# Four 64x64 tiles for the score columns of a graph-attention kernel, from a copy with exchanged partition halves, at the end of the step

## The chip, the cores and the metric

The kernel runs on one core of one Trainium2 chip. The metric is the device time of one launch in microseconds (us), the median of several runs. A profile is one further execution; its span goes from the first to the last instruction and leaves out what lies around them.

## The reference, cut to what matters

Eight batches of 2048 nodes with 64 channels go through two graph-attention layers under one mask (a random adjacency plus the diagonal), then a leaky ReLU, a layer norm with gamma and beta, the residual and a second layer norm.

```python
def _gat_layer(h, mask, b):
    scores = jnp.einsum('...nd,...md->...nm', h, h)
    scores = jnp.where(mask, scores, NEG)
    attn = jax.nn.softmax(scores, axis=-1)
    return jnp.einsum('...nm,...md->...nd', attn, h) + b
h = jnp.einsum('bnc,hdc->bhnd', x, Wh)              # 4 heads of 64
out_h = _gat_layer(h, mask[None, None], bh[None, :, None, :])
z = jax.nn.leaky_relu(cat, negative_slope=0.2)      # cat: the heads side by side
h2 = jnp.einsum('bnk,dk->bnd', z, Wo)
out2 = _gat_layer(h2, mask[None], bo)
z2 = jax.nn.leaky_relu(out2, negative_slope=0.2)
out = layernorm(z2) * gamma + beta
x = layernorm(x + out)
```

## The kernel before

The adjacency is sparse apart from the first 59 nodes ("hubs"). The other 1989 nodes are split into 153 sets of 13. For each set the kernel finds the up to 128 neighbours of its members, gathers their rows from a table in DRAM with an indirect DMA, and does the attention of the set on that block. The 8 batches stand as 4 pairs (Q), the two batches of a pair in the two halves of the 128 partitions (channels 0 to 63 of the one, 64 to 127 of the other).

A score of layer 1 is x_n' (Wh' Wh) x_m for each head. So the kernel first multiplies the own rows of a set by the 64x64 matrix Wh'Wh of each head. These products are the **score columns**. `gram` holds the four matrices as 128x128 blocks with the same 64x64 matrix in both diagonal quarters and zeros elsewhere, so that one 128x128 matmul serves both batches of a pair.

Layer 1 runs as one loop of steps i, each for a group of two sets (77 groups). All order is written by hand; the engines execute their own instructions in that order and wait for each other by semaphores. A step does, for several groups at different stages:

- `scores(i + 1)` (L901): 32 matmuls of 64x64 tiles, gathered rows against the columns y; `weigh` (L906, VectorE) subtracts the mask, `lift` (L913, ScalarE) takes exp.
- `project` (L579): the heads' weights on the attention output of group i - 1, 64x64 tiles, into the PSUM tile `cat`; `leaky` (L566, ScalarE) moves it to z, `leak` (L571, VectorE) follows.
- the ScalarE copies of the two transposed banks to xTg (L1235).
- `values(i)` (L927) into `o`; `invert` (L934, L935, VectorE) divides by the sums into `osb`.
- `second_maps` (L961) and `second_rows` (L971), both into other columns of `cat`; VectorE keeps them with `keep_own` (L966) and `keep_rows` (L975), and two DMAs on SP's queue store the rows in the second layer's table (L978).
- `columns(i + 4)` (L886): two matmuls (four records, for fp32 takes two passes) of 128x128 tiles on 208 columns into `cat`; `keep_columns` (L892, ScalarE) copies them to y.
- `turn` of the rows of the group three on, first set (L560, four transposes into bank 0), `turn_values(i)` (L944, four transposes of `osb`), `keep_values` (L951, two ScalarE copies), `turn` of the second set (L560, bank 1).

On every even step GpSimd makes the own rows of four sets (`own_rows`, L880, tile `xo`, two buffers), for the columns of the step two on and of the one after it. `cat` has one buffer: the next step's `project` writes into it only when all readers of the last one are through.

SP's queue issues DMAs in order. From step 30 on every even step adds the twelve or so loads of own rows of x (L1010) and the store of the last ones with beta (L1015) to the two row stores of each step; the loads wait until the store from the same buffer, issued just ahead of the last two row stores, has landed. Before that step it has the row stores, and in the first steps the rest of the adjacency loads.

## Time and profile before

| | |
|---|---|
| median of 3 runs | 963.1 us (962.69 to 968.35) |
| span of the profiled execution | 828.9 us, granted TensorE clock 0.974 |
| difference of median and span, outside the profile | 134.2 us |
| busy share: TensorE matmul, VectorE, ScalarE, GpSimd | 87%, 72%, 64%, 54% |
| chain that ended last: TensorE, VectorE, DMA | 61%, 13%, 12% |
| layer 1 loop | from 138.6 us to about 566 us of the span |
| a regular step of it | 5.13 to 5.14 us |

The page has no time of the profiled execution other than the span; the times of runs are device times of other executions. A row of the timeline reads: start, duration, engine, line, operation, tile written <- tiles read, shape of the tile and of the operands, count, and in brackets the idle time ahead and what ended it. The end of a matmul is modelled, so neighbouring rows overlap by a little; starts are recorded. A row of the chain reads: start, time charged, what. "PEld" is the load of the weights.

### The profile page before, as it was taken

How to read it: one execution, taken by the hardware profiler on the slowest of the kernel's cores; microseconds unless marked ns; L12 is line 12 of the kernel's file. 1: busy time of each engine (PE TensorE's matmuls, PEld its weight loads, DVE VectorE, ACT ScalarE, POOL GpSimd, SP SyncE). 2: the span in 40 equal slices, each digit the busy share in tenths (PEclk: the TensorE clock that was granted, in tenths of full speed). 3: DMA queues.
4: the chain of work that ended last, by engine and by line, in shares of the span. 5: the costliest groups of instructions: out<-in, count | busy, mean ns of one | idle time of the engine just before them, and what ended most of it. 6: DMA issues, size and time to landing. Idle time of an engine off the chain costs nothing.

```text
span 828.9 us, 40381 instructions
## 1 busy us (share of the span) xinstructions
PE 725.0 (87%) x17262; PEld 615.5 (74%) x17262; DVE 600.8 (72%) x1328; ACT 529.3 (64%) x1131; POOL 449.9 (54%) x620
## 2 busy tenths in 40 slices
PE   1998688889999999999999999998999899989820
PEld 1675457678788889898989889887787688877620
DVE  3446984568778877898767777764347999998883
ACT  0354445556666667667667667773667899988852
POOL 5455356456445455555545555512777777777600
PEclk9999999999999999999999999999999999999975
DMA  4988744343323333454545545532986667766621
GB/s 83 231 225 240 219 156 111 98 121 98 86 71 90 96 90 98 119 144 139 143 120 141 142 139 137 142 114 88 300 245 185 192 170 214 224 201 197 172 54 32
DMA packets 80262, 121.55 MB, mean 147 GB/s; under 512 B 34539, under 2 KB 50751, under 8 KB 80075
## 3 DMA queue, kind: packets, MB, share of 16 engines
q0 software_dynamic: 24752, 65.67, 29.4%
q1 hardware_dynamic: 50973, 52.11, 21.6%
q8 instruction: 138, 2.26, 1.1%
q10 hardware_dynamic: 4350, 1.10, 0.7%
q14 instruction: 49, 0.40, 0.2%
HBM read 116.81 MB, written 18.25 MB: 163 GB/s over the span
## 4 chain that ended last, share of the span: by engine, by line
PE 61%; DVE 13%; DMA 12%; ACT 5%; issue 4%; SPq 3%; POOL 1%; POOLq 0%; DVEq 0%; ACTq 0%
PE s L901 10%; PE o L927 10%; PE bank L560 8%; PE cat L886 6%; DMA raw<-in_adj_dram 4%; PE o L944 4%; PE cat L579 4%; PE cat L961 4%; PE t L560 3%; PE bank L1343 2%; SPq L1461 2%; PE cat L971 2%; PE o L1373 2%; DMA rows<-table,index 2%; DMA out_dram<-y_s 2%
## 5 line engine op out<-in xcount | busy, mean ns | idle before, releaser
L872 POOL DMA_INDIRECT g<-table,index x154 | 162.3, 1054 | 172.8 <-PE o L927 145.5
L872 POOL DMA_INDIRECT rows<-table,index x153 | 161.2, 1053 | 51.8 <-issue 18.6
L566 ACT ACTIVATE z<-cat,bhp 128x208 f32<-128x208 f32 x154 | 58.4, 430 | 101.7 <-PE cat L579 101.7
L906 DVE TENSOR_TENSOR e<-s,mask 128x832 f32<-128x832 f32 x77 | 78.6, 1020 | 28.4 <-PE s L901 27.6
L927 PE MATMUL o<-g,e 128*64 128x65 f32 x2464 | 92.3, 226 | 5.6 <-issue 5.5
L560 PE MATMUL t<-ident,rows 128*128 128x128 f32 x612 | 86.1, 278 | 10.0 <-DMA rows<-table,index 4.7
L560 PE MATMUL bank<-ident,g 128*128 128x128 f32 x616 | 92.3, 273 | 1.5 <-DVE e L1106 1.2
L927 PEld LDWEIGHTS o<-g,e 128*64 128x64 f32 x2464 | 80.1, 138 | 17.1 <-issue 6.9
L901 PE MATMUL s<-y,xTg 64*64 64x52 f32 x4928 | 88.7, 220 | 0.0
L901 PEld LDWEIGHTS s<-y,xTg 64*64 64x64 f32 x4928 | 78.9, 134 | 12.9 <-issue 12.9
L1497 ACT COPY xts<-t 128x512 f32<-128x512 f32 x153 | 82.2, 583 | 7.0 <-PE t L560 6.0
L1235 ACT COPY xTg<-bank 128x512 f32<-128x512 f32 x154 | 82.6, 596 | 2.4 <-PE bank L560 2.4
L560 PEld LDWEIGHTS t<-ident,rows 128*128 128x128 f32 x612 | 66.5, 140 | 23.0 <-issue 9.9
L913 ACT ACTIVATE e<-e,shifts 128x832 f32<-128x832 f32 x77 | 78.4, 1019 | 2.0 <-DVE e L906 2.0
L742 POOL TENSOR_SCALAR a<-raw 117x1024 bf16<-117x1024 int32 x34 | 38.7, 1140 | 71.5 <-DMA raw<-in_adj_dram 49.1
L560 PEld LDWEIGHTS bank<-ident,g 128*128 128x128 f32 x616 | 73.5, 140 | 4.9 <-issue 1.3
L657 ACT ACTIVATE e<-e,shifts 128x960 f32<-128x960 f32 x32 | 35.1, 1096 | 54.7 <-DVE e L654 49.0
L886 PE MATMUL cat<-xo,gram 128*128 128x208 f32 (+1 forms) x304 | 66.3, 341 | 0.8 <-issue 0.8
L951 ACT COPY otb<-o 128x208 f32<-128x208 f32 x154 | 43.8, 335 | 22.0 <-ACT y L892 10.9
L654 DVE TENSOR_TENSOR e<-sh,maskh 128x960 f32<-128x960 f32 x32 | 36.9, 1154 | 26.6 <-PE sh L650 17.2
L935 DVE TENSOR_TENSOR osb<-o,rall 128x512 f32<-128x512 f32 x77 | 53.2, 692 | 2.7
L934 DVE RECIPROCAL rall<-o 64x8 f32<-64x8 f32 x154 | 31.5, 204 | 31.7 <-PE o L927 30.2
(198 smaller groups left out, 1488.0 us busy)
## 6 DMA issues: line engine op xcount, KB each, us to landing
raw<-in_adj_dram SPq DMA_DIRECT2D x34, 432.0 KB
xr_s<-table SPq DMA_DIRECT2D x19, 256.0 KB
table<-x SPq DMA_DIRECT2D x16, 260.0 KB
table<-rowt SPq DMA_DIRECT2D x152, 26.4 KB
out_dram<-y_s SPq DMA_DIRECT2D x152, 24.0 KB
x<-in_x_dram SPq DMA_DIRECT2D x24, 128.0 KB
table<-xb SPq DMA_DIRECT2D x11, 256.0 KB
table<-share SPq DMA_DIRECT2D x10, 256.0 KB
```

Of the source, the lines that this page charges most:

```text
L560: nc.tensor.transpose(tp[:, q * P:(q + 1) * P], rows[:, q, 1:1 + P], ident)
L566: nc.scalar.activation(z[:, hp], cat[:, :, hp * n:(hp + 1) * n], AF.Identity, bias=bhp[:, hp:hp + 1], scale=1.0)
L872: nc.gpsimd.indirect_dma_start(out=t.rearrange("n q c -> n (q c)"), out_offset=None, in_=table, in_offset=bass.IndirectOffsetOnAxis(ap=ind ...
L886: nc.tensor.matmul(cat[:, k, :n], gram[:, g % 2 * 2 + k, :], held["x", g // 2][:, :n], start=True, stop=True)
L901: nc.tensor.matmul(sp[half(r), p, (q * 2 + j) * M:(q * 2 + j + 1) * M], xt[half(p), j, q, half(r)], y[half(p), (j * Q + q) * M:(j * Q + q ...
L906: nc.vector.tensor_tensor(e[:, :16 * M].rearrange("p (a q n) -> p a q n", a=2, q=Q), sp[:, :, :8 * M].rearrange("p a (q n) -> p a q n", q= ...
L913: nc.scalar.activation(e[:, :16 * M], e[:, :16 * M], AF.Exp, bias=shifts[:, 0:1], scale=1.0)
L927: nc.tensor.matmul(op[half(p), j, o0:o0 + K1], e[:, c0:c0 + 64], rw[j][:, q, sums(p)], start=True, stop=True)
L935: nc.vector.tensor_tensor(osb, v[:, :, :, 1:K1], r.unsqueeze(3).to_broadcast([P, 4, 2, D]), OP.mult)
L951: nc.scalar.copy(ot.rearrange("c h (p w n) -> c p h w n", p=2, w=4)[:, p], v[:, :, p * 64:p * 64 + M].rearrange("c w (n h) -> c h w n", h=H))
L1235: nc.scalar.copy(t[:, k, :], bank[k])
L1497: nc.scalar.copy(xts[pair(s) % 4][:, s % 2, :], tp)
```

## The change

The columns of a head pair are made by four 64x64 matmuls in place of two 128x128 ones, one for each head and each batch of the pair. Head k of the pair reads row half k of the array and writes PSUM bank k, for both output halves p. Where k and p are the same half, the moving data are the own rows `xo` as they stand; where they differ, they come from `xs`, a copy of `xo` with the two partition halves exchanged. `swap_rows` makes that copy with two DMAs on SP's queue (each 64 partitions of 832 bytes), at the end of every odd step, for the columns of the next step and of the one after it. `xs` has one buffer. The columns and their copy to y move from the middle of the step, behind `second_rows`, to its end, behind the second `turn`. To make room, two tiles of the hub nodes take parts of a shared tile in place of buffers of the work pool.

```diff
+    def swap_rows(m):
+        n = quad(m)[1] * Q * SET
+        t = held["xs", m] = work.tile([P, 2 * GM], F32, tag="xs", name=f"xs{m}", bufs=1)
+        for k in range(2):
+            nc.sync.dma_start(out=t[half(k), :n], in_=held["x", m][half(1 - k), :n])
...
+    def columns_by_halves(g, cat):
+        n = quad(g // 2)[1] * Q * SET
+        for off in range(2):
+            for k in range(2):
+                p = k ^ off
+                nc.tensor.matmul(cat[half(p), k, :n], gram[half(k), g % 2 * 2 + k, half(k)],
+                                 held["xs" if off else "x", g // 2][half(k), :n], start=True, stop=True)
...
+    swap_rows(1)
...
             second_rows(i - 3, pr)
-        if 2 <= i + 4 < NG + NG % 2:
-            columns(i + 4, cat)
-            keep_columns(i + 4, cat)
...
             turn(bank[1], rows[1, 2 * (i + 3) + 1])
+        if 2 <= i + 4 < NG + NG % 2:
+            columns_by_halves(i + 4, cat)
+            keep_columns(i + 4, cat)
+            if i % 2 and i + 5 < NG + NG % 2:
+                swap_rows((i + 5) // 2)
```

TensorE in an even step of the loop before, from the second layer's maps to the next scores (`cat` is the PSUM tile of projection, maps and columns, `o` that of the values, `bank` those of the transposed rows, `g` gathered rows):

```order
L961 MATMUL cat_8030<-z_7930,woT 64x2x4x13 [waits Activation_49]
L961 MATMUL cat_8030<-z_7930,woT 64x2x4x13 x3
L971 MATMUL cat_8030<-ident,own_7975 104x128
L886 MATMUL cat_8030<-xo_7840,gram 128x208 [waits Pool_49]
L886 MATMUL cat_8030<-xo_7840,gram 128x208
L560 MATMUL bank_1919<-ident,g_106_7832 128x128 [waits DMASW7_49,Activation_49]
L560 MATMUL bank_1919<-ident,g_106_7832 128x128 x3
L944 MATMUL o_8046<-ident,osb_8063 128x116 [waits DVE_49]
L944 MATMUL o_8046<-ident,osb_8063 128x116 x3
L560 MATMUL bank_1920<-ident,g_107_7836 128x128 [waits DMASW0_49,Activation_49]
L560 MATMUL bank_1920<-ident,g_107_7836 128x128 x3
L901 MATMUL s_8124<-y_7862,xTg_8042 64x52 [waits PE_49]
```

The same place in the changed kernel (its lines L976, L986, L900, L959 and L916 are the maps, the rows, the columns, the turned values and the scores):

```order
L976 MATMUL cat_8211<-z_8106,woT 64x2x4x13 x3
L986 MATMUL cat_8211<-ident,own_8148 104x128
L560 MATMUL bank_1919<-ident,g_106_8006 128x128 [waits DMASW7_49,Activation_49]
L560 MATMUL bank_1919<-ident,g_106_8006 128x128 x3
L959 MATMUL o_8227<-ident,osb_8244 128x116 [waits DVE_49]
L959 MATMUL o_8227<-ident,osb_8244 128x116 x3
L560 MATMUL bank_1920<-ident,g_107_8010 128x128 [waits DMASW0_49,Activation_49]
L560 MATMUL bank_1920<-ident,g_107_8010 128x128 x3
L900 MATMUL cat_8211<-xo_8014,gram 64x208 [waits DVE_49,Pool_49]
L900 MATMUL cat_8211<-xo_8014,gram 64x208
L900 MATMUL cat_8211<-xs_8174,gram 64x208 [waits DMAHW1_49]
L900 MATMUL cat_8211<-xs_8174,gram 64x208 [waits DMAHW2_49]
```

The columns went from between `second_rows` and the first transposes to behind the second ones; between `second_rows` and the transposes of `osb` only four transposes are left. The second pair of matmuls waits for the two DMAs of the copy; in odd steps it has no wait of its own.

SP's queue in the changed kernel, from step 30 on, from the row stores of an even step to the loads of the next one (`rowt` are rows for the second layer's table, `table_174` takes the own rows with beta, `xb` is one of the two tiles for own rows):

```order
L993 DMA table_99<-rowt_113 4x13x130 [waits DMAHW4_49,DVE_49]
L993 DMA table_99<-rowt_113 4x13x130 [waits DMAHW5_49]
L1030 DMA table_174<-xb 128x512 [waits DMAHW6_49,DVE_49]
L993 DMA table_99<-rowt_114 4x13x130 [waits DMAHW7_49,DVE_49]
L993 DMA table_99<-rowt_114 4x13x130 [waits DMAHW0_49]
L886 DMA xs_8174<-xo_8014 64x208 [waits DMAHW1_49,PE_49,Pool_49]
L886 DMA xs_8174<-xo_8014 64x208 [waits DMAHW2_49]
L1025 DMA xb<-in_x_dram 12x2x256 [waits DMAHW6_49,DMAHW3_49]
```

The two DMAs of `xs` are new, between the odd step's row stores and the next loads; the rest is as before. The first of them waits for TensorE, which must be through with the last `xs`, and the loads behind it still wait for the store into `table_174` to land.

ScalarE, before and then changed, from the exp of a step to the next step's projection:

```order
L913 ACTIVATE e_111<-e_111,shifts 128x832 [waits DVE_49,Activation_49]
L892 COPY y_8572<-cat_8505 128x208x2 [waits PE_49]
L951 COPY otb_8590<-o_8521 128x4x52 [waits DVE_49,PE_49,Activation_49]
L951 COPY otb_8590<-o_8521 128x4x52
L566 ACTIVATE z_8640<-cat_8631,bhp 128x208 [waits PE_49]
```

```order
L928 ACTIVATE e_111<-e_111,shifts 128x832 [waits DVE_49,Activation_49]
L966 COPY otb_8536<-o_8471 128x4x52 [waits DVE_49,PE_49,Activation_49]
L966 COPY otb_8536<-o_8471 128x4x52
L907 COPY y_8547<-cat_8455 128x208x2 [waits DVE_49,PE_49]
L565 ACTIVATE z_8592<-cat_8583,bhp 128x208 [waits PE_49]
```

The copy of the columns to y went from ahead of the two copies of the turned values to behind them, so it is the last thing that ScalarE reads from `cat` before the next projection writes there.

## Prediction

> **What bounds the kernel now.** First the page: the engines' busy shares and the chain that ended last.

> ```profile
> PE 725.0 (87%) x17262; PEld 615.5 (74%) x17262; DVE 600.8 (72%) x1328; ACT 529.3 (64%) x1131; POOL 449.9 (54%) x620
> PE 61%; DVE 13%; DMA 12%; ACT 5%; issue 4%; SPq 3%; POOL 1%; POOLq 0%; DVEq 0%; ACTq 0%
> ```

> TensorE is the busiest engine and most of the chain, but over the whole span. So the chain inside the loop comes next, for one regular step.

> ```profile
> 403.16 1.08 PE s L901 x64
> ...
> 404.24 0.37 PE cat L579 x16
> 404.61 1.08 PE o L927 x32
> ...
> 406.32 0.71 PE cat L886 x4
> 407.02 0.44 PE bank L560 x4
> 407.46 0.40 PE o L944 x4
> ...
> 408.30 1.08 PE s L901 x64
> ```

> The step is TensorE from end to end: 408.30 - 403.16 = 5.14 us, of which the columns (L886) are 0.71. If nothing else moved, every 0.1 us off TensorE's work would be 0.1 us off the step. The timeline of the same step says whether something else stands close behind.

> ```profile
> 404.54 1.15 PE L927 MATMUL o<-g,e 128*64 128x65 f32 x32
> ...
> 405.74 0.42 DVE L934 RECIPROCAL rall<-o 64x8 f32<-64x8 f32 x2 [0.41 <-PE o L927]
> ...
> 406.15 0.87 PE L886 MATMUL cat<-xo,gram 128*128 128x208 f32 x4
> 406.20 0.69 DVE L935 TENSOR_TENSOR osb<-o,rall 128x512 f32<-128x512 f32 x1
> ...
> 407.30 0.56 PE L944 MATMUL o<-ident,osb 116*128 116x116 f32 x4
> ...
> 407.69 0.60 PE L560 MATMUL bank<-ident,g 128*128 128x128 f32 x4
> ...
> 408.23 0.39 PE L901 MATMUL s<-y,xTg 64*64 64x52 f32 x11
> ```

> VectorE waits for the end of the values (L927), takes two reciprocals and the division into osb, and is through at 406.20 + 0.69 = 406.89. TensorE reads osb at 407.30 (L944). So the slack is 0.41 us, and it exists because the columns (L886, 0.71 in the chain) lie between. **The second bound is this path, values, reciprocals, osb, turned values, and it starts and ends on TensorE.**

> The trace shows what happens without that cover. Late in the loop the columns are half as wide, and then there are none.

> ```profile
> 542.21 1.15 PE L927 MATMUL o<-g,e 128*64 128x65 f32 x32
> ...
> 543.82 0.59 PE L886 MATMUL cat<-xo,gram 128*128 128x104 f32 x4
> ...
> 544.68 0.26 PE L944 MATMUL o<-ident,osb 116*128 116x116 f32 x1
> ...
> 551.92 1.15 PE L927 MATMUL o<-g,e 128*64 128x65 f32 x32
> ...
> 554.33 0.61 PE L944 MATMUL o<-ident,osb 116*128 116x116 f32 x4 [0.63 <-DVE osb L935]
> ```

> From the start of the values to the turned values it is 407.30 - 404.54 = 2.76 us in a regular step, 2.47 with half columns and 2.41 with none, where TensorE waits for osb. The last figure doesn't depend on what TensorE has to do meanwhile: **2.41 us is the floor.** (In that case the four transposes of bank 0 are missing too; they are 0.44 in the chain, less than the 0.63 of the wait without them, so with them the floor stands.)

> **The change, part by part.** *Taking the columns out of the middle.* TensorE's work there falls by 0.71, but the leg falls only from 2.76 to 2.41: a gain of 0.35 us a step, and a new wait for osb of about 0.35. That wait replaces the cover.

> *Refilling after the wait.* [...] After the wait the next operation's matmul starts 560.14 - 559.69 = 0.45 behind the first turned value, against 407.69 - 407.30 = 0.39 in the regular step: 0.06 lost.

> ```profile
> 559.69 0.61 PE L944 MATMUL o<-ident,osb 116*128 116x116 f32 x4 [0.63 <-DVE osb L935]
> 560.14 0.27 PE L1174 MATMUL bank<-share,own 128*117 128x120 f32 x1
> ```

> *The columns at the end.* Four matmuls of 64x64 tiles, 208 columns, two records each: 8 records. The projection is 16 records of 104 columns in the same four quarters of the array, as many record columns, and the chain above charges it 0.37. The hub scores are the nearest row in width:

> ```profile
> 127.43 1.04 PE L650 MATMUL sh<-share,xT 64*64 64x240 f32 x16
> L650 PE MATMUL sh<-share,xT x512: 362/363/660, 28.4 to 130.5; 64*64 64x240 f32 x171
> ```

> Sixteen records of 240 columns, the last one 0.36 long: three groups of four in 0.68, 0.23 a group, and 2 groups x 0.23 x 208/240 = 0.39. Below, four exact groups without any start-up are 0.35 (half of the 0.71); above, two at a time, 0.71. I take 0.37. The switch from the transposes' shape to 64x64 tiles is paid now ahead of the scores and then ahead of the columns: no term.

> *Sum of a regular step:* -0.35 + 0.06 + 0.37 = **+0.08 us**. With 0.35 for the columns it is +0.06. The steps are counted by the scores between 185 and 535 us, the stretch of regular steps with full columns (first row, 64 records a step); the second row, of the chain, is a stop of TensorE between the maps:

> ```profile
> L901 PE MATMUL s<-y,xTg 64*64 64x52 f32 x4160 | 74.8, 220 | 0.0
> ...
> 537.98 0.22 issue
> ```

> 4160 / 64 = 65 steps: +4 to +5 us. Where TensorE stops for another reason between values and turned values, as in the second row, the wait for osb is hidden, and the step gains up to 0.34. I count some eight such steps, by stops and by the adjacency work that stands there in three steps: -2 us. The first five steps, bound by VectorE and ScalarE, and the two with half columns cost together about as much as they gain.

> *ScalarE.* The copy to y goes behind the turned values' copies, and the next projection may write `cat` only behind it.

> ```profile
> 407.16 0.55 ACT L892 COPY y<-cat 128x416 f32<-128x416 f32 x1
> ```

> By the terms above the columns start 3.4 us behind the values' start, their last record ends 0.23 + 0.34 later, the copy takes 0.55: 4.6. The projection is due at 3.4 + 0.37 + 0.97 of scores = 4.74. It holds with some 0.15 to spare; nothing is charged, but the bound is 0.1 a step (+7 us) if starts come later than I reckon. What hides the copy is the scores alone.

> *VectorE.* The columns now wait for its two reads of `cat`. Where osb is waited for, the second one reads:

> ```profile
> 554.86 0.28 DVE L975 TENSOR_TENSOR rowt<-cat,bob 104x128 f32<-104x128 f32 x1
> ```

> It ends at 555.14, 0.81 behind the turned values' start (554.33); the columns come 0.45 + 0.54 (the transposes, 408.23 - 407.69) behind that start: no wait, 0.17 to spare.

> *The copy of the own rows.* Two DMAs every two steps. Through step 29 SP's queue has little else, and the copy has a step of 5.1 us to land in. From step 30 on it is this:

> ```profile
> 407.74 5.54 SPq L1010 DMA_DIRECT2D xb<-in_x_dram  x12
> ...
> 414.79 0.41 SPq L1015 DMA_DIRECT2D table<-share  x1
> 415.30 1.24 SPq L978 DMA_DIRECT2D table<-rowt  x2
> 418.60 0.72 SPq L1010 DMA_DIRECT2D share<-in_x_dram  x2
> ```

> The queue runs late by itself: the loads of step 46 start 4.6 us after its scores (403.16), the odd step's row stores end at 416.54, and its loop, 418.60 - 407.74 = 10.9 us, is a little over two steps. The copy comes at 416.6 and takes two issues of about 0.62, as the row stores do. No row shows a DMA from SBUF to SBUF; the nearest landing is the first row here, and behind it stands the time that the queue has to spare, which is its wait for the store of L1015 to land ahead of the next loads (total, times, longest):

> ```profile
> 570.23 2.48 DMA table<-rowt
> ...
> SPq L1010 <- DMA table<-xb: 13.2, 9, 2.8
> SPq L1010 <- DMA table<-share: 10.0, 8, 2.5
> ...
> 419.65 0.55 PE s L901 x27
> ```

> With that 2.5 us for the landing the copy is in place at 416.6 + 1.25 + 2.5 = 420.3. The columns of step 48 would be due 0.4 ahead of the scores at 419.65: the copy is 1.0 late. The queue doesn't wait for TensorE at that point, so one such wait shifts TensorE against the queue for good, and it comes again only as far as SP's loop is the longer one. The spare time is (13.2 + 10.0) / 17 = 1.36 us a loop against 1.25 of new issue: hidden on the average, not in each loop, since single waits differ (up to 2.8). Where the spare is short, the loop grows by the rest; for about a third of some 19 loops at 0.7 that is 4 us, and I charge **+4.5 us** with the first shift, less what TensorE's own slower steps give back. The bounds are 0 (the copy lands at once; it can only add waits, so there is nothing below) and +21 (the first rival).

> [...]

> **The sum.** 828.9 + 4.5 (regular steps) - 2 (stops) + 4.5 (late copies) = 835.9 us of span. With the 134.2 us between the span and the median of the runs unchanged, that is 963.1 + 7 = **970 us**, 0.7% more.

> **The rivals.** *The copy sets SP's loop and so the step* (slower). If the copy lands behind the 256 KB store in the same queue, and the store later for it, the whole 1.25 us comes on top: 10.7 becomes about 11.8 us for two steps, and TensorE follows from step 30 to 71: 19 pairs x 1.1 = +21, in place of 4.5, 986 us. It decides from the point where the spare time falls under the issue, which is close: 1.36 against 1.25. Against it: SP starts out with TensorE at step 30 and has some 2 us until it is late. Chance 0.14.

> *Columns two at a time* (slower): 0.34 more in 74 steps, +25, 995 us. Chance 0.08.

> *The wait for osb doesn't come* (faster): the whole 0.71 - 0.37 = 0.34 is kept in 70 steps, -24, and the copies still come late: 943 us. It would need VectorE to end osb 0.35 earlier behind the values; its three operations are 1.1 us in every step shown and start when the values end. Chance 0.10. That the new order is not what runs is excluded by the order shown above.

> **How the numbers follow.** The forecast has 0.68. About 1% is what a measurement of this kernel can tell from no change (its three runs spread over 0.6%): below 953.5 or above 972.7. The forecast's own range, from the terms' bounds (columns 0.35 to 0.45, copy 0 to 10, ScalarE 0 to 7), is 961 to 984, so about 0.16 of its 0.68 is slower by over 1%. Faster 0.10, slower 0.14 + 0.08 + 0.16 = 0.38, within 1% 0.52. The range of 8 in 10 takes in the first rival's 986 and leaves out the other two: 957 to 988.

> **What would show it.** In a regular step of the changed kernel: a wait of 0.2 to 0.4 us ahead of L959 put down to osb; columns of about 0.37 with scores right behind; a step of about 5.2. In even steps from 30 on, waits ahead of the third column matmul for the DMA of xs, few if I am right, in each if the first rival is. Projections waiting for the copy to y would show ScalarE's term. Wrong altogether I would be if osb came earlier, or if the columns hid in time that the scores leave unused.

## The result, and the profile after

The changed kernel takes 989.1 us (median of 4 runs, 987.2 to 990.2) against 965.7 for the kernel before on the same chip: **ratio 1.025, 95% interval 1.021 to 1.029, slower.** Forecast was 970, with a range up to 988.

One thing must be known ahead of any row. The kernel before takes 966 to 976 us in four sets of runs and 829 in the other two; the runs of one set share a chip. Its page in the prediction (span 828.9) is of the quicker sort, its median of 963.1 of the slower. So rows are compared here within one sort: "quicker" and "slower" chip. The record numbers the chip of each set of experiments: both quicker sets ran on chip 10, the slower ones on chips 6 (twice) and 8; that of the first, slower set isn't on record. So it goes with the chip; what makes the difference isn't shown. In the loop it is not the granted clock, which is 1.00 from 340 to 540 us on the old page and on that of e1.

On the slower chip, the heads of the pages: first the kernel before (run e1), then the changed one (from an earlier set).

```profile
span 975.8 us, 40381 instructions
PE 803.1 (82%) x17262; PEld 656.8 (67%) x17262; DVE 604.1 (62%) x1328; ACT 529.3 (54%) x1131; POOL 445.2 (46%) x620
PE 61%; DVE 10%; issue 8%; DMA 8%; POOL 4%; ACT 3%; another core or an unknown queue 3%; SPq 2%; ACTq 0%; DVEq 0%; POOLq 0%
```

```profile
span 988.4 us, 41175 instructions
PE 790.3 (80%) x17566; PEld 627.7 (64%) x17566; DVE 593.6 (60%) x1328; ACT 533.3 (54%) x1131; POOL 439.3 (44%) x620
PE 49%; DVE 15%; issue 11%; DMA 8%; ACT 5%; POOL 4%; another core or an unknown queue 3%; SPq 2%; DVEq 0%; POOLq 0%; ACTq 0%
```

TensorE is less busy, as meant, and is 49% of the chain where it was 61%. VectorE, ScalarE and "issue" (time in which the engine waits for nothing that the profile shows) have taken its place. From the scores of step 0 to those of step 72 the loop takes 439.1 us against 413.9 in e1, 25.2 more, where the times differ by 23.4. (The two spans differ by less because they are of two sets, whose times for the kernel before are 10 us apart.) On the quicker chip the loop takes 430.2 us (e13) against 399.3 on the old page: 30.9 of the 31.3 us by which the spans differ. So the loss lies in the loop.

The chain of a regular step on the quicker chip (run e13) shows the change as it was meant:

```profile
318.39 0.92 PE s L916 x64
319.31 0.37 PE cat L578 x16
319.68 1.11 PE o L942 x32
...
321.27 0.70 DVE osb L950
321.98 0.04 issue
322.02 0.61 PE o L959 x4
322.63 0.44 PE bank L560 x4
323.07 0.51 PE cat L900 x8
323.59 0.92 PE s L916 x64
```

The step is 323.59 - 318.39 = 5.20 us. The turned values come 322.02 - 319.68 = 2.34 behind the values' first piece in the chain, straight behind osb, and the columns end where the scores begin.

Where the rest went is seen when the time from each TensorE record's start to the next one's is added up by operation, in steps 30 to 71 (42 steps, worked out from the traces' records):

| us in 42 steps | predicted change | quicker: before, e13 | change | slower: e1, changed | change |
|---|---|---|---|---|---|
| wait for osb, and turned values | +17.2 (0.41 a step) | 17.3, 33.3 | +16.0 | 17.2, 34.2 | +17.0 |
| columns, with the steps to and from them | -14.3 (0.34 a step) | 45.6, 48.3 | +2.7 | 44.7, 36.0 | -8.7 |
| of it, waits for the copy | up to +4.5 | 0, 15.8 | +15.8 | 0, 2.9 | +2.9 |
| values | 0 | 44.0, 52.2 | +8.2 | 41.2, 49.4 | +8.2 |
| scores, and to the projection | 0 | 40.8, 43.7 | +2.9 | 55.2, 59.3 | +4.1 |
| all of the step | | 221.7, 252.3 | +30.6 | 233.6, 254.4 | +20.8 |

(The waits for the copy are the time inside the columns, 26.7 and 13.5, less that of runs without such waits, 10.9 in e16 and 10.6 in e17.) The first two terms are as forecast once those waits are taken out. The others are not. Of the 8.2 us in the values, 6.7 on the quicker chip and 7.5 on the slower are stops of over 0.25 us between two records; e9 and e14 show what these are.

### The profile page after: what moved, and what is told of

Same layout as the page of the kernel before. It is cut to its first block, busy times and chain, and to the rows that moved or that the text cites. A ratio compares the mean times of both kernels' runs of the same rounds, so it can differ in the third digit from the quotient of the medians.

```text
span 988.4 us, 41175 instructions
## 1 busy us (share of the span) xinstructions
PE 790.3 (80%) x17566; PEld 627.7 (64%) x17566; DVE 593.6 (60%) x1328; ACT 533.3 (54%) x1131; POOL 439.3 (44%) x620
## 4 chain that ended last, share of the span: by engine, by line
PE 49%; DVE 15%; issue 11%; DMA 8%; ACT 5%; POOL 4%; another core or an unknown queue 3%; SPq 2%; DVEq 0%; POOLq 0%; ACTq 0%
PE o L942 8%; PE s L916 6%; PE t L560 5%; PE bank L1361 5%; PE bank L560 4%; PE o L959 4%; PE cat L900 4%; POOL rows L871 3%; PE cat L578 3%; DMA raw<-in_adj_dram 2%; PE o L1391 2%; DVE osb L950 2%; DMA x<-in_x_dram 2%; DVE share L800 2%
## 5 line engine op out<-in xcount | busy, mean ns | idle before, releaser
L560 PE MATMUL t<-ident,rows 128*128 128x128 f32 x612 | 93.5, 283 | 16.3 <-issue 9.3
L916 PEld LDWEIGHTS s<-y,xTg 64*64 64x64 f32 x4928 | 100.0, 135 | 10.4 <-issue 6.9
L916 PE MATMUL s<-y,xTg 64*64 64x52 f32 x4928 | 102.0, 221 | 4.1 <-issue 3.2
L560 PE MATMUL bank<-ident,g 128*128 128x128 f32 x616 | 93.3, 275 | 4.6 <-DVE keysi L829 1.6
L560 PEld LDWEIGHTS t<-ident,rows 128*128 128x128 f32 x612 | 68.5, 143 | 36.5 <-issue 26.7
L966 ACT COPY otb<-o 128x208 f32<-128x208 f32 x154 | 43.6, 335 | 79.1 <-PE o L959 29.8
L1361 PE MATMUL bank<-xts,share 128*32 128x128 f32 x1224 | 62.2, 278 | 18.9 <-issue 15.1
L560 PEld LDWEIGHTS bank<-ident,g 128*128 128x128 f32 x616 | 71.9, 142 | 6.6 <-DVE keysi L829 2.0
L1361 PEld LDWEIGHTS bank<-xts,share 128*32 128x32 f32 x1224 | 37.1, 109 | 41.3 <-issue 35.3
L959 PE MATMUL o<-ident,osb 116*128 116x116 f32 x308 | 47.4, 277 | 14.0 <-DVE osb L950 7.3
```

Source lines behind the costliest of these rows:

```text
L560: nc.tensor.transpose(tp[:, q * P:(q + 1) * P], rows[:, q, 1:1 + P], ident)
L916: nc.tensor.matmul(sp[half(r), p, (q * 2 + j) * M:(q * 2 + j + 1) * M], xt[half(p), j, q, half(r)], y[half(p), (j * Q + q) * M:(j * Q + q ...
L959: nc.tensor.transpose(turned(op)[:, w, :], osb[:RC, w].rearrange("a s c -> a (s c)"), ident[:RC, :RC])
L966: nc.scalar.copy(ot.rearrange("c h (p w n) -> c p h w n", p=2, w=4)[:, p], v[:, :, p * 64:p * 64 + M].rearrange("c w (n h) -> c h w n", h=H))
L1361: nc.tensor.matmul(sp[q * 32:(q + 1) * 32, k, :], bd[u % 3][:, k, q, :], xt[:, s % 2, q, :], start=True, stop=True, tile_position=(0, q * 32))
```

## The experiments

**e1: the kernel before, for a page of the slower chip.**

> The kernel before, unchanged. Its profiled execution had a span of 828.9 us and 134 us outside it, the changed kernel's has 988.4 us and 2 us outside. Theory (the old page shows a quicker execution than the timed ones): a new profile has a span of some 961 us, with the same 5.14 us step in the loop, and the second layer takes as long as with the change, about 378 us, where the old page has 252. Rival (the change slows the second layer as well): the span is again near 829, and 126 us of second layer are the change's. Ratio of the times 1.00 in both.

Ratio 1.0007 (0.997 to 1.005); span 975.8 with a time of 977.8. The old page was the quicker one: what the prediction took for 134 us outside the span is inside it, most of it behind the loop: from the last scores on (583.2 us here, 556.8 there) it is 393 us in place of 272. The step is longer too, 5.2 to 5.8 us in most steps from 30 on, not 5.14:

```profile
346.53 0.44 PE bank L560 x4
346.97 0.49 PE s L901 x22
347.46 0.21 issue
347.67 0.89 PE s L901 x36
```

The scores stop in the middle for no shown reason. And ScalarE's copies of the turned values wait for TensorE three times as long (waits of the old page, then of e1; total, times, longest):

```profile
ACT otb L951 <- PE o L944: 8.4, 19, 1.9
```

```profile
ACT otb L951 <- PE o L944: 25.3, 27, 1.9
```

**e2: four tiles and the copy at the columns' old place.**

```diff
         if 0 <= i - 3 < NG:
             second_rows(i - 3, pr)
+        (columns_by_halves, keep_columns, swap_rows as at the step's end)
```

> Four tiles and the copy of the own rows, but at the columns' old place in the middle of the step. Theory A (the move does it: the copy to y stands behind the turned values' copies, and the next projection waits for it): with the move undone the 24 us are gone, 960 to 968 us; only the wait for osb of 0.35 us a step remains, which takes the place of the 0.35 us that the columns save. Theory B (the copy by two DMAs does it, it sets SP's loop from step 30 on): 980 to 990 us, as slow as the change.

1.013 (1.008 to 1.018): half of the loss is left, so neither theory has all of it. Many odd steps take 5.09 to 5.10, even ones up to 7.4, waiting for the copy (13 us in all from step 30 on). And in the middle the tiles save next to nothing: from the start of L986 to that of the turned values it is 0.247 + 0.514 + 0.493 = 1.254 us where the old columns have 0.155 + 0.705 + 0.437 = 1.297. Matmuls of 128 rows stand on both sides there, and the step from them to 64x64 tiles costs about 0.09 more than between equal shapes, and the step back as much (0.267 against 0.176 us from the last column to the next start).

**e3: old columns, no copy, at the step's end.**

```diff
-            columns_by_halves(i + 4, cat)
+            columns(i + 4, cat)
             keep_columns(i + 4, cat)
-            if i % 2 and i + 5 < NG + NG % 2:
-                swap_rows((i + 5) // 2)
```

> The old columns, 128x128 with 0.71 us, and no copy of the own rows, but at the step's end. Theory A (the move does it): slower than the changed kernel by up to the 0.34 us in 70 steps that its columns are shorter, 989 to 1013 us. Theory B (the copy by DMA does it): the step is longer by 0.71 - 0.35 = 0.36 us, 75 times, and nothing else, 990 us with a step of 5.5 in all stretches, even and odd steps alike, with turned values' copies that start 0.34 us behind the last transpose as before.

1.022 (1.016 to 1.028). Through step 29 the step is 5.63 to 5.69, or 147.8 us in 25 steps against 139.1 in e1: +0.35 a step, theory B's 0.36. From 30 on many odd steps are at about 6.05, which B doesn't explain; 998 us lies in theory A's range too. The move alone is dear, with or without tiles.

**e4 and e16: no copy.**

```diff
-        for k in range(2):
-            nc.sync.dma_start(out=t[half(k), :n], in_=held["x", m][half(1 - k), :n])
+        nc.vector.memset(t, 0.0)      (once, for all steps)
```

> The changed kernel without the copy of the own rows: the two tiles that read it read zeros set once, so two of the four score columns are zero. Theory A (the move does it): 980 to 990 us, no quicker than the changed kernel by more than 1%. Theory B (the copy by DMA sets SP's loop): the slow steps from 30 on go back to 5.2 us, about 965 to 970 us.

> The changed kernel without the copy of the own rows (two of the tiles read zeros set once, so two of the four score columns are zero; behind the two layers this makes the kernel run its path for dense rows as well, so only the loop of its profile counts). If the late copy costs what was reckoned, its loop from step 0 to step 72 is 4 to 6 us shorter than that of the changed kernel on the same chip; if it sets SP's loop, 20 us.

The times, 7315.7 and 7182.5 us, hold the kernel's path for dense rows, which runs behind the two layers here; only the loops count. On the slower chip it is 432.7 against 439.1 us, 6 less; on the quicker one 417.6 against 430.2 (e13), 13 less. The copy costs about what was reckoned (4.5) on one chip; on the other it lies halfway between that and the first rival's 21.

**e5 and e8: the copy a step earlier, with two buffers, at the end and in the middle.**

```diff
-        ... tag="xs", name=f"xs{m}", bufs=1)
+        ... tag="xs", name=f"xs{m}", bufs=2)
+        if i + 6 < NG and i % 2 == 0 and i >= -2:
+            swap_rows((i + 6) // 2)          (behind load_own)
-            if i % 2 and i + 5 < NG + NG % 2:
-                swap_rows((i + 5) // 2)
```

> The changed kernel with two buffers for the copy (and two instead of three for z, which makes room), so that it is issued a step earlier, behind the loads of the even step. Theory A (of the loop's 25 us the wait for osb is 0.35 a step, the projection's wait for the copy to y 0.11, and the late copy only some 5 us in all): the ratio falls from 1.025 to about 1.02. Theory B (the copy sets SP's loop): no gain, since SP issues as much as before; 1.025 or more, with loads and row stores that are later still.

> Four tiles at the old place in the middle, with the copy issued a step earlier (two buffers). In the middle, even steps wait 0.6 to 1.4 us for the late copy, odd steps took 5.10. Theory A: without the wait all steps are like the odd ones, and the ratio falls from 1.013 to 1.00. Theory B (SP's issue itself is the cost): stays at 1.013.

This edit, like those of e7, e8, e12, e17 and e18, also takes the tile z from three buffers to two, for room.

1.031 (1.023 to 1.039) and 1.018 (1.012 to 1.024): a miss of theory A. In e5 the copy is on time (33.0 us for the columns in 42 steps, 36.0 with the change), but the loop is no shorter, 443.5 us: its steps from 5 to 29 take 146.4 us in place of 141.9, for which the trace shows no cause. In e8 the copy still comes late:

```profile
PE cat L900 <- DMA xs<-xo: 6.0, 6, 3.1
```

```profile
456.76 8.23 SPq L1025 DMA_DIRECT2D xb<-in_x_dram  x14
465.11 1.19 SPq L886 DMA_DIRECT2D xs<-xo  x2
```

The copy stands behind the loads, which SP starts late. These loads are those of step 50, and the copy is issued 1.6 us into step 52, whose columns read it. In the middle of the step the columns are due earlier than at its end, where e5 has the copy on time: from step 30 on they lose 15 us to it in e8. SP's waits for GpSimd's own rows are not the cause: from there on they are 2.5 us in all.

**e6 and e15: bank 1 ahead of the turned values, the leak behind VectorE's reads of `cat`.**

```diff
-            turn(bank[0], rows[1, 2 * (i + 3)])
+            for j in range(2):
+                turn(bank[j], rows[1, 2 * (i + 3) + j])
         if 0 <= i < NG:
             turn_values(i, op)
             keep_values(i, op)
-        if 0 <= i + 3 < NG:
-            turn(bank[1], rows[1, 2 * (i + 3) + 1])
...            (and leak(held["z", i - 1]) from ahead of keep_own and keep_rows to behind them)
```

> The changed kernel with the transposes of bank 1 ahead of the turned values instead of behind them, and the leak on VectorE behind its two reads of cat instead of ahead of them. Theory A (TensorE's own work is less with the tiles, but 0.35 us a step go to the wait for osb): the wait is filled by 0.44 us of transposes, the step is about 0.3 shorter than the changed kernel's 5.2, and the time falls to 0.99 to 1.00 of before. Rival (VectorE and ScalarE bound the step: the copies of the turned values and to y end when they end): no change, 1.02 to 1.03.

> Bank 1's transposes ahead of the turned values and the leak behind the two reads of cat, again. On the slower chip 1.02, as before. On the quicker one, where the signal that the turned values are done comes 0.34 us behind them, TensorE's order should set the step: about 4.9 to 5.0 us in place of 5.14, ratio 0.98 to 1.00; 1.01 or more if the copies behind the turned values bind there too.

1.023 (1.016 to 1.029) on the slower chip, 1.025 (1.018 to 1.032) on the quicker one. The wait for osb is gone in both (17.2 us in place of 34.2 and 33.3). On the slower chip the scores take it back, 73.2 us in place of 59.3, in stops with no cause shown:

```profile
L916 PE MATMUL s<-y,xTg 64*64 64x52 f32 x4928 | 110.8, 220 | 23.7 <-issue 23.2
```

On the quicker chip many steps up to 29 are 4.8 to 5.1, the shortest of any run (134.7 us from step 5 to 30, before 138.9), and from 30 on the copy takes it back: some 30 us inside the columns. This is the row of e15 and, for comparison, of e13 (steps 30 to 71):

```profile
PE cat L900 <- DMA xs<-xo: 19.8, 19, 3.3
```

```profile
PE cat L900 <- DMA xs<-xo: 8.3, 11, 1.9
```

**e7: both edits (e5 and e6).**

> Both edits of the two runs ahead. Theory A: the gains add up, 0.98 to 0.995 of before. Rival (ScalarE's chain binds): 1.02.

1.024 (1.018 to 1.031), slower chip: the gains don't add up, as with e5 and e6 alone.

**e9 and e10: without the own rows' loads, the changed kernel and the one before.** The edit takes out `load_own((i - 30) // 2)`.

> The changed kernel without the loads of the own rows of the second layer (SP, from step 30 on; the buffers keep ones, so the second layer's own rows are not added). Theory C (in the steps from 30 on TensorE's signal that the turned values are done comes 1.2 to 1.9 us late, because those loads are under way, and the chain signal, two copies of the turned values, copy to y, projection sets the step): the signal comes 0.34 to 0.7 us behind, steps of 5.2 to 5.4, the loop from the scores of step 0 to those of step 72 about 410 us instead of 442, ratio 0.99 to 1.00. Rival (the loads have no part in it): 1.02 to 1.03, with the signal as late as before.

> The kernel before without those loads. Theory C: its steps from 30 on fall from 5.4 to 5.7 us to 5.14 to 5.35, the loop from 417 to about 403 us, ratio 0.985, and the changed kernel without loads is then no more than 1% slower than this one. Rival: 1.00.

1.019 (1.014 to 1.025) and 0.998 (0.995 to 1.001), both on the quicker chip, where ScalarE starts on the turned values 0.34 us behind them in any case, so theory C stays open, and neither ratio is the one that it foretold. They tell something else. With SP's queue empty the copy is on time (33.0 us for the columns, as without a copy), regular steps are 5.19 and 5.22, and yet the changed kernel is 2% slower. Most of what is left is in the values: 51.7 us against 43.9 in the 42 steps, of 11.7 in all. The timeline of e9 there:

```profile
441.39 1.13 PE L916 MATMUL s<-y,xTg 64*64 64x52 f32 x64
442.31 0.58 PE L578 MATMUL cat<-otb,whT 64*64 64x104 f32 x16
442.83 0.74 PE L942 MATMUL o<-g,e 128*64 128x65 f32 x17
445.18 0.62 PE L942 MATMUL o<-g,e 128*64 128x65 f32 x14 [1.62 <-issue]
```

TensorE stops in the middle of the values (1.62 us), waiting for nothing that the profile shows. If its instructions (weight loads, matmuls and waits) are counted from the start, 15 of the loop's 16 such stops (over 0.3 us from one weight load to the next) stand at place 193 or 194 modulo 256; so do 13 of 15 in the old page of before. They are up to 1.93 us long. The page's third part has the queue that carries instructions (packets, MB):

```profile
q8 instruction: 140, 2.29, 1.2%
```

2.29 MB in 140 packets is 16.4 KB each; 17,566 matmuls and as many weight loads in about 140 packets are, as an estimate, 250 instructions a packet. In the eight stops that leave the matmuls idle for over 0.5 us from 340 us on, TensorE goes on 2.3 to 2.6 us behind the start of such a packet.

**e14: the changed kernel with the stream shifted by 128 instructions.**

```diff
+    for _ in range(32):
+        nc.tensor.matmul(bank[0][:, :2], ident, ident[:, :2], start=True, stop=True)
```

> The changed kernel with 32 small matmuls (128 instructions of TensorE) once ahead of the loop. A regular step has 284 instructions, 28 more than 256, so a fixed place modulo 256 wanders through the step and is in the values (instructions 160 to 224 of a step) in two or three steps of every nine: 34 to 36, 43 to 45, 52 to 54, 61 to 63, 70 to 72. Theory (the pauses are TensorE's wait for the next block of 256 instructions): with the stream shifted by 128 they stand in steps 30 and 31, 39 and 40, 48 and 49, 57 and 58, 66 and 67, and the former ones are free of them. Rival (they belong to what those steps do, searches, gathers or loads): the same steps pause as before.

1.061 (1.049 to 1.074). Again 10 of 11 stops are at 193 or 194 modulo 256, now in other steps. In e13 steps 16 to 18 have them (0.56, 1.14 and 0.74 us); in e14 these take 5.19, 5.21 and 6.74, and the stops stand in 13 and 14, 21 to 23, 47 to 50 and 65. Those of 21 to 23:

```profile
285.01 0.39 PE L942 MATMUL o<-g,e 128*64 128x65 f32 x5 [0.78 <-issue]
...
290.64 0.74 PE L942 MATMUL o<-g,e 128*64 128x65 f32 x18 [0.59 <-issue]
...
298.00 0.34 PE L578 MATMUL cat<-otb,whT 64*64 64x104 f32 x2 [2.46 <-issue]
```

Behind 27 of the 32 values, then behind 14, then behind 14 of the 16 projections that come ahead of them: 13 and 16 matmuls earlier, about the 14 that 28 instructions make. The stops belong to the instruction stream, not to what a step does. Of the five places foretold, one (48 and 49) has it in full, and at 30, 39 and 57 there is none, for which no cause is shown. The 32 matmuls cost 11 us ahead of the loop.

**e11: the copy to y on VectorE. e12: tiles in the middle, the copy issued by ScalarE.**

```diff
-            keep_columns(i + 4, cat)
+            keep_columns(i + 4, cat, nc.vector.tensor_copy)
```

```diff
+            nc.scalar.dma_start(out=t[half(k), :n], ...)     (behind keep_values of the even step)
```

> The changed kernel with the copy to y on VectorE instead of ScalarE. Theory C: the projection no longer waits for two copies and a third behind them, it comes up to 0.45 us earlier in the steps from 30 on, ratio 1.005 to 1.015. Rival (VectorE's search for the next links stands ahead of the copy and makes it as late): 1.02 to 1.03.

> Four tiles at the old place in the middle, the copy with two buffers issued by ScalarE at the end of the even step, behind the turned values' copies, so that SP's lateness has no part in it. Theory (in the middle only the late copy costs): no waits for the copy, steps of 5.1 to 5.5 as in the odd steps of the run with tiles in the middle, ratio 0.99 to 1.005. Rival (two issues of 0.6 us hold up ScalarE's copies behind the projection): 1.01 to 1.02.

1.062 (1.053 to 1.070) and 1.035 (1.026 to 1.043), quicker chip. Both rivals hold in kind, and both runs are slower than these said: in e11 the projection waits 15.7 us in 42 steps for the copy on VectorE (2.6 in e13); in e12 the copy is on time (10.7 us inside the columns), but from the values to the maps it is 22.0 us (2.1 in the old page), most of it put down to z, which ScalarE's two issues and its one buffer less can both make late.

**e13: the changed kernel on the quicker chip.**

> The changed kernel, unchanged. 1.02 to 1.03 on a chip like the one of its first runs; on the quicker chip (829 us for the kernel before) steps of 5.19 and 5.22 where nothing else intervenes, as in the run without loads, and 1.015 to 1.025.

1.042 (1.033 to 1.051), a miss: worse than foretold and than on the slower chip, where the copy costs less. Up to step 29 it is as fast as before (137.3 us from step 5 to 30, before 138.9). Then the chain runs over the copy and SP:

```profile
328.99 0.58 SPq L993
...
329.69 4.38 DMA xs<-xo
```

```profile
SPq L1025 <- DMA table<-share: 6.4, 7, 2.0
SPq L1025 <- DMA table<-xb: 4.9, 6, 1.5
```

The copy takes 4.38 us from issue to landing here, ten of the 21 even steps from 30 on wait over 0.2 us for it (two on the slower chip), and SP's spare time ahead of the loads is down to 11.3 us, from 23.2.

**e17 and e18: the copy by GpSimd, with the changed order and with e6's.**

```diff
             own_rows((i + 6) // 2)
+            swap_rows((i + 6) // 2)          (with nc.gpsimd.dma_start and two buffers)
```

> The changed kernel with two buffers for the copy, issued by GpSimd right behind the own rows (and two instead of three buffers for z, for room). Theory (SP's queue makes the copy late): no waits for it in the even steps from 30 on, the loop 12 to 16 us shorter than the changed kernel's on the quicker chip, ratio 1.02 to 1.03 there (1.02 on the slower one). Rival (GpSimd's issue of about 1 us each holds up the gathers, and values wait for rows instead): 1.04.

> Bank 1 ahead of the turned values, the leak behind the reads of cat, and the copy by GpSimd. Theory: on the quicker chip steps of 4.75 to 5.0 throughout, where the run with SP's copy had them up to step 30, ratio 0.97 to 0.99, faster than both kernels; on the slower chip, where the copies behind the turned values bind, 1.01 to 1.02. Rival (GpSimd): 1.02 or more on either chip.

1.015 (1.006 to 1.024) and 1.013 (1.005 to 1.021), slower chip. No wait for the copy is left, and the loop of e17 is 9 us shorter than the changed kernel's (430.1 against 439.1, of another set). Whether e18 would beat the kernel before on the quicker chip was not seen: both runs came on the slower one. No version here is faster than the kernel before.

## Why the prediction was wrong, point by point

- **The bound and the floor: right.** The turned values follow osb at the floor in nearly every step; wait and refill cost 16.0 and 17.0 us where 17.2 were worked out.
- **Columns at the end, four at once: right.** Without the copy's waits the columns fall by 13.1 and 11.6 us, worked out 14.3. Two at a time, as in the second rival, they would have taken up to 0.71 a step by the prediction's estimate; no run shows that. In e13 the tiles from `xs` start 0.02 us behind those from `xo`, though each head's two read the same row half of the array:

```profile
323.00 0.39 PE L900 MATMUL cat<-xo,gram 64*64 64x208 f32 x2
323.02 0.39 PE L900 MATMUL cat<-xs,gram 64*64 64x208 f32 x2
```

- **The regular step: right,** 5.19 and 5.22 where 5.14 + 0.08 was said. That stops give 2 us back isn't shown: e13 is 1.5 us quicker than before from step 5 to 30, but because its values stop less there (25.6 against 28.6 us), not because a wait is hidden.
- **The copy of the own rows: mis-sized.** The term was 4.5 us, with 2.5 us for the landing and 1.36 us of spare time in SP's loop. The landing took 2.89 us in a chain of the changed kernel on the slower chip and 3.60 and 4.38 in two of e13, and the cost is 13 to 16 us on the chip from whose page the term was read (6 on the other). What the first rival would show, a wait in each even step, stands in ten of 21 there and in two on the slower chip: on the quicker the truth lay between forecast and rival, on the slower near the forecast.
- **Not in the sum at all: TensorE's stops at fixed places of its instruction stream,** most of the +8.2 us of values on either chip (6.7 and 7.5). The change adds 8 instructions a step and puts columns, scores, projection and values in one dense row of 240. Whether that brings the stops on is open: e6 and e15 have the same count and row, and such stops of 0.9 us and none in the values of these steps. The old page had these stops ("0.22 issue" is one of this kind in the chain); the prediction took them for a place where the step could gain.
- **ScalarE: 1 us on the quicker chip (2.6 us from scores to projection in e13, 1.6 before), +5.0 us on the slower (7.0 against 2.0),** within the bound of 7 that was named and not charged. There ScalarE starts on the turned values up to 1.6 us (e1) or 1.9 us (changed) behind the start of their last record in most steps from 30 on, 0.34 where nothing is late; in the changed one the copy to y stands behind those copies, and the projection behind it. The chain of the changed kernel:

```profile
377.00 0.34 ACT otb L966
377.34 0.44 ACT y L907
377.78 0.04 issue
377.83 0.59 PE cat L578 x16
```

- **The base: wrong.** The 134.2 us "outside the span" were the difference of two chips. As a share, 7 us are 0.8% of 829; that alone would have moved the forecast by 1 us, but it hid that a step measured at 5.14 was not the timed one.
- **The range: added up wrong.** The bounds that it names (columns 0.35 to 0.45, copy 0 to 10, ScalarE 0 to 7) give 964 to 988 around 970, not 961 to 984. The measured 989 lies outside of both.

So the steps that failed are two terms taken as nothing, TensorE's stops in its instruction stream and ScalarE's copy, and one that was too small, the late copy. For the slower chip, that of the timed runs, they add up to 8.2 (all of the values) + 5.0 + about 2 = 15 us more than the forecast of +7, which leaves 1 us to the measured 23. On the quicker one the rows of the table give for steps 30 to 71, 16.0 - 13.1 + 15.8 + 8.2 + 2.9 = 29.8 of 30.6 us. ScalarE's part is borne out by the other runs on slower chips: from scores to projection it is 5.9 to 7.3 us where the columns and their copy to y stand at the step's end (the changed kernel, e3, e4, e5, e17), and 2.0 to 3.1 where they stand in the middle (e1, e2, e8).

## What to carry to other kernels

The cover taken away from VectorE's path showed up as a wait of about the same length (16 to 17 us, 17.2 worked out), and that could be priced from the trace. Two more losses came with the change that were not priced, or too low: the values, with TensorE's stops in them (8 us), and the late queue (3 to 16 us). Before a transfer is added to a queue that runs late, see when its data are due: an earlier place in the same queue was enough for the end of the step (e5), not for its middle (e8). Other queues had it on time as well, GpSimd's (e17) and ScalarE's, the latter at the price of ScalarE's own work (e12). And compare the profiled span with the timed runs first: the gap of 14% here (828.9 against 963.1 us) came from a page and times of two chips; in e1, of one execution, it is 2 us.
